# Moving a variance off VectorE, and loading a slot's weights one slot ahead, in a selective-scan kernel

## The chip, the cores and the metric

The kernel runs on one core of one Trainium2 chip. A core has a matrix engine (TensorE, PE in the profile), three engines for elementwise work (VectorE is DVE, ScalarE is ACT, GpSimd is POOL), and SyncE (SP), whose queue issues most of the transfers between HBM and the on-chip memory SBUF. TensorE writes its results to PSUM, a small memory in banks. Each engine takes its own instructions in order; semaphores order them across engines. The metric is the time of one execution on the device, in microseconds (us). Lower is better.

## What is computed

The input is 8 images of 128 x 128 tokens with 128 channels. Layer 0 is linear attention with a layer norm. Layer 1, where the change lies, expands each token to 256 channels (called `Cd` in the reference), runs a depthwise convolution, and then four scans over the image: by rows, by rows backwards, by columns, by columns backwards. Their sum is gated, normalised over the 256 channels and projected to 128. Cut to what matters:

```python
delta = softplus(dt_out + dbias)             # per channel and token
xc = exp(delta * A) * xc + (delta * u) * B   # the scan, token after token
y_k = xc * C + u * D                         # k = 0..3, one for each direction
y = y0 + y1 + y2 + y3                        # each turned back to the image's order
yz = y * silu(z)
mu = yz.mean(-1, keepdims=True)
var = ((yz - mu) ** 2).mean(-1, keepdims=True)
out = (gamma * (yz - mu) / sqrt(var + 1e-05) + beta) @ Wout
```

The kernel takes the variance as mean(yz^2) - mean(yz)^2, clamps it at zero and adds 1e-5.

## The kernel before

Three stages run one after the other: `layer0`, `layer1_front` (projection, convolution, the rows from which delta, B and C come) and `layer1_scan`. The change lies in the last one, which begins at about 4970 us of 9860 us. Inside the block `in_order` each engine's instructions keep the order in which the program writes them.

**Units, slots, images.** The scans are cut into 512 units of 1024 tokens (`CH`). Sixteen units in a row (`NCH`) make a slot: one image and one of its four directions. Four slots in a row add into one output image `o`, in a buffer `y` that holds the whole image; the first slot of an image has place 0. `step(n)` writes the work around unit n, with stages of neighbouring units interleaved by hand.

**A unit.** `load_rows` brings the rows that `delta` multiplies on TensorE by the slot's weights `dw` (L873, into a tile `px`, one of three in PSUM). ScalarE takes softplus of it (`soften`, L877), then exp (`decay`, L881). GpSimd multiplies delta into the input (`weigh`, L884). VectorE scans both halves of the channels (`scan`, L891 or L893). `spread` (L907) copies C over the partitions on TensorE, and in the next step `emit` (L919, L924, L931, L935) multiplies by it, with `gather` (L943, VectorE) and `add` (L950, GpSimd) adding to `y` in the slots of place 1 to 3. Softplus and exp need different activation tables, so each step has two table loads on ScalarE (counted under L877 and L881).

**Leaving.** When an image is complete, its 16 tiles of 1024 tokens leave one a step, while the first slot of the next image overwrites `y` behind them. For a tile: `gate` multiplies `y` by z one step ahead, one half on GpSimd and one on VectorE (L970); `square` (L973, ScalarE) squares it in place; `moments` (L983, TensorE) sums both over the channels; `keep` (L989, ScalarE) copies these rows from PSUM; `to_tokens` (L995, TensorE) turns them so that each token lies on a partition, in a tile `pq` of 8 means and 8 mean squares per partition; `variance` (L997 to L1003, VectorE) makes the variance; `deviation` (L1006, GpSimd, in the next step) raises it to -1/2; `project` (L1013, TensorE) multiplies by the output weights; `store` (L1019, VectorE, in the next step) scales by the deviation and sends the rows out. `moments`, `to_tokens` and the second `spread` share one PSUM buffer, called "pt", one after the other. A *leaving step* below is a step in which a tile passes `square` to `variance`: 7 x 16 of them beside scans and 16 more at the end, after the last scan.

**Weights.** A slot's weights are ten small transfers (`weights`, L813 and L814) into one of two buffers that alternate between slots. They stand in SyncE's queue just ahead of the rows of the slot's first unit, which is two steps ahead of that unit.

**Order in a step.** For VectorE in a leaving step: first scan, the stores of the tile ahead, second scan, the state (L901), the variance (L999 to L1003), the gate of the next tile (L970), then, in the next step's text, the two halves of the emit (L919). For ScalarE: both decays, both squares, `keep`, both softenings for the next unit. For GpSimd: `weigh` of the first half, `deviation`, `weigh` of the second half, `gate`, and in some steps a transfer that adds a part of the sums into `y` (L844).

Of the kernel before, what the change touches and what calls it, by code (L numbers as in the profile page):

```python
# [8 lines left out]
F32 = mybir.dt.float32  # L9
BF16 = mybir.dt.bfloat16  # L10
AF = mybir.ActivationFunctionType
ALU = mybir.AluOpType
# [4 lines left out]
P = 128  # L17
# [4 lines left out]
NC2 = 2  # L22
R = 8
K = 4
GW = 4
# [6 lines left out]
NCH = L // CH  # L32
EPS0 = 1e-3
EPS1 = 1e-5
# [26 lines left out]
@contextmanager  # L61
def in_order(tc):

    bb = tc.nc.cur_bb
    first = len(bb.bb.instructions)
    yield
    assert tc.nc.cur_bb is bb
    info = mybir.DependencyInfo(mybir.DependencyClass.NoSync, mybir.DependencyReason.DATA)
    last = {}
    for i in bb.bb.instructions[first:]:  # L70
        if i.engine in last:
            tc.add_manual_dep(i, last[i.engine].name, info, reason="in_order")
        last[i.engine] = i
# [614 lines left out]
def layer1_scan(ctx: ExitStack, tc, ubs, xps, zs, gs, dtw, dtb, a_log, gamma, beta, w_out, out):  # L688
# [15 lines left out]
    nc = tc.nc  # L704
# [3 lines left out]
    sm = ctx.enter_context(tc.tile_pool(name="l2s", bufs=4))  # L708
# [31 lines left out]
    half = const.tile([P, GW, 2], F32, name="half2")  # L740
    nc.vector.memset(half, -0.5)
    rws, dws = [], []
    for i in range(3):
        t = const.tile([P, CH], BF16, name=f"rows{i}")
# [3 lines left out]
    for i in range(2):  # L748
        t = const.tile([P, D2], BF16, name=f"dtw{i}")
# [83 lines left out]
    units = []  # L833
    for o in range(B):
        for s in ([3, 0, 1, 2] if o % 4 < 2 else [1, 2, 3, 0]):
            sl = Slot(len(units) // NCH, o, s)
# [9 lines left out]
    def load_rows(n):  # L846
        sl, i = units[n]
        m = sl.at(i)
        if i == 0:
            sl.weights()  # L850
        rw = rws[n % 3]
        md = NCH - 1 - m if sl.dt_turned_back else m
        src = xps[sl.dt_image, sl.dt_order].rearrange("j r l -> (j r) l")
        for j in range(3):
            nc.sync.dma_start(rw[3 * NR * j : 3 * NR * j + 3 * NR, :], src[:, md * CH : md * CH + CH])
        nc.sync.dma_start(rw[96:99, :], xps[sl.b, sl.order, :, R + 1, m * CH : m * CH + CH])

    def load(n):
        sl, i = units[n]
        m = sl.at(i)  # L860
        ubt[n] = wp.tile([P, NC2, CH], F32, name="ubt", tag="ub", bufs=4)
        nc.sync.dma_start(ubt[n], ubs[sl.b, sl.order].rearrange("c p l -> p c l")[:, :, m * CH : m * CH + CH])
# [16 lines left out]
    def decay(n, c):  # L879
        sl, i = units[n]  # L880
        nc.scalar.activation(da[n, c], sp[n, c], AF.Exp, scale=sa[:, sl.s, c : c + 1])  # L881

    def weigh(n, c):
        nc.gpsimd.tensor_tensor(ubt[n][:, c, :], ubt[n][:, c, :], sp.pop((n, c)), ALU.mult)  # L884

    def scan(n, c):
        sl, i = units[n]
        x, e = da[n, c], ubt[n][:, c, :]
        start = 0.0 if i == 0 else st[n - 1][:, c : c + 1]
        if sl.back:  # L890
            nc.vector.tensor_tensor_scan(e[:, ::-1], x[:, ::-1], e[:, ::-1], start, ALU.mult, ALU.add)  # L891
        else:
            nc.vector.tensor_tensor_scan(e, x, e, start, ALU.mult, ALU.add)  # L893
# [43 lines left out]
    def gather(n):  # L937

        sl, i = units[n]
        v = sl.y_at(i, 0)  # L940
        if sl.y_turned:
            v = v.rearrange("p c a b -> p c b a")
        nc.vector.tensor_tensor(v, v, ts.pop(n), ALU.add)  # L943
# [6 lines left out]
            nc.gpsimd.tensor_tensor(v[:, c], v[:, c], h[:, c], ALU.add)  # L950


    zt, rst, pts = {}, {}, {}

    def piece(m, hf):
        return y[:, :, (2 * m + hf) * GN : (2 * m + hf + 1) * GN]
# [15 lines left out]
    def square(m, hf):  # L972
        nc.scalar.activation(piece(m, hf), zt[m, hf], AF.Square)  # L973
# [17 lines left out]
    def to_tokens(m):  # L991
        sr = pts.pop((m, "rows"))
        pts[m] = p = pe.tile([P, GW, NC2, 2], F32, name="pq", tag="pt")
        for w in range(GW):
            nc.tensor.matmul(p[:, w], sr[:, w * H : w * H + H], sel, start=True, stop=True)  # L995

    def variance(m):  # L997
        mv = sm.tile([P, GW, NC2, 2], F32, name="mv")
        nc.vector.tensor_copy(mv, pts.pop(m))  # L999
        rst[m] = rstd = sm.tile([P, GW, NC2], F32, name="rstd")  # L1000
        nc.vector.tensor_tensor(rstd, mv[:, :, :, 0], mv[:, :, :, 0], ALU.mult)
        nc.vector.tensor_tensor(rstd, mv[:, :, :, 1], rstd, ALU.subtract)
        nc.vector.tensor_scalar(rstd, rstd, 0.0, EPS1, ALU.max, ALU.add)  # L1003

    def deviation(m):
        nc.gpsimd.tensor_tensor(rst[m], rst[m], half, ALU.pow)  # L1006

    def project(m, hf, bank):
        z = zt.pop((m, hf))
# [18 lines left out]
    for o in range(B):  # L1028
        n = (o + 1) * K * NCH
# [5 lines left out]
    N = len(units)  # L1035

    def step(n):
        live = 0 <= n < N
        then = n + 1 < N
        before = 1 <= n <= N  # L1040
        now, last, soon = (leaving.get(n + i) for i in (0, -1, 1))
        first = before and units[n - 1][0].place == 0
        if before:
            emit(n - 1, 0)
            if not first:
                gather(n - 1)
            emit(n - 1, 1)
        if n + 2 < N:
            load_rows(n + 2)
        if first and n + 3 < N:  # L1050
            load(n + 3)
        if live:
            for c in range(NC2):
                decay(n, c)
            weigh(n, 0)
        if last:
            deviation(last[1])
        if live:
            weigh(n, 1)
        if now:  # L1060
            for hf in range(2):
                square(now[1], hf)
            moments(now[1])
        if live:
            scan(n, 0)
            da.pop((n, 0))
        if last:
            for hf in range(2):
                store(*last, hf)
        if then:  # L1070
            for c in range(NC2):
                delta(n + 1, c)
        if now:
            keep(now[1])
        if then:
            for c in range(NC2):
                soften(n + 1, c)
        if now:
            to_tokens(now[1])
        if live:  # L1080
            scan(n, 1)
            state(n)
        if now:
            variance(now[1])
        if live:
            spread(n, 0, "pc")
            spread(n, 1, "pt")
        if soon:
            gate(*soon, 0, nc.gpsimd)
            gate(*soon, 1, nc.vector)  # L1090
        if now:
            p = da.pop((n, 1)) if live else px.tile([P, CH], F32, name="px")
            for hf in range(2):
                project(now[1], hf, p[:, hf * 512 : hf * 512 + 512])
        elif live and units[n][0].place == 0:
            da.pop((n, 1))
        if before and not first:
            add(n - 1)
        if n + 3 < N and not first:
            load(n + 3)  # L1100
        if n in summed:
            add_d(*summed[n])
        if n in fetched:
            fetch(*fetched[n])

    with in_order(tc):
        for n in range(2):
            load_rows(n)
        for n in range(3):
            load(n)  # L1110
        for c in range(NC2):
            delta(0, c)
            soften(0, c)
        for n in range(N + NCH + 1):
            step(n)
# [65 lines left out]
```

## Time and profile before

The time before is 9870.49 us, the median of 3 runs (9860.43 to 9883.38). The profiled execution spans 9860.3 us. What matters of it:

| part | what | us |
|---|---|---|
| scans L891 and L893, VectorE | 960 with a carried state, 64 without | 2355.3 |
| weigh L884, GpSimd | 1024, mean 2431 ns | 2442.4 |
| soften L877, ScalarE | 1024, mean 1024 ns, and 512 table loads of 1283 ns | 1035.4 + 656.9 |
| decay L881, ScalarE | 1024, mean 1109 ns, and 512 table loads of 1283 ns | 1103.1 + 656.9 |
| variance L999, L1001, L1002, L1003, VectorE | 128 each, means 165, 825, 677 and 223 ns | 242.1 |
| gate L970, VectorE half | 128, mean 1261 ns | 161.5 |
| deviation L1006, GpSimd | 128, mean 2326 ns | 297.8 |
| the seven leaving phases with scans | 112 steps | 1383.7 |
| after the last scan | 16 leaving steps | 150.3 |

The page gives an instruction a line of the kernel, an engine, its tiles (out<-in), its shape, how often it runs, and the engine's idle time just before it with what ended it. "Busy" includes the time in which an instruction has been started and waits inside for a memory port; only an idle gap says that an engine had nothing to start. An engine can therefore look full without working. Comparing the minimum, the median and the maximum of one shape shows such waiting.

### The profile page before, as it was taken

To read this page: it belongs to the slowest core of one execution; us is meant where nothing else is said; L and a number is where in the kernel's file an instruction comes from. 1 tells how busy PE (TensorE), PEld (TensorE's weight loads), DVE (VectorE), ACT (ScalarE), POOL (GpSimd) and SP (SyncE) were. 2 spreads that over 40 slices of the span, in tenths; PEclk is the share of its full clock that TensorE was granted. 3 is DMA by queue.
4 is the path that set the end of the run, shared out by engine and by line. 5 is a ranking of instruction groups with operands and counts; after the bars stand their busy time and mean duration, and the time that the engine had idled before them with its cause. 6 is when DMAs were issued, how large, how long until landed. Compare 5 with 4: busy or idle time off the path is not lost. (4 is left out here: it accounts for less than half of the span.)

```text
span 9860.3 us, 90189 instructions
## 1 busy us (share of the span) xinstructions
PE 6392.8 (65%) x24352; PEld 3116.9 (32%) x24352; DVE 8364.1 (85%) x9060; ACT 7121.7 (72%) x8098; POOL 7143.2 (72%) x4224
## 2 busy tenths in 40 slices
PE   8889999988787678766733644536345363543636
PEld 5555555553232223222200311304023040220403
DVE  6556775566898888888889999999999999999996
ACT  5556565556877777777778787787877878777784
POOL 3444554455584568766769899898988989889897
PEclk9999999999898889888855756757567585665857
DMA  2332223323675678877755957769486684866848
GB/s 91 130 129 108 85 109 128 131 101 140 218 229 211 226 259 240 233 250 255 259 164 159 261 157 219 211 171 254 151 230 197 179 249 152 246 182 192 236 152 216
DMA packets 1034809, 1851.22 MB, mean 188 GB/s; under 512 B 274852, under 2 KB 500772, under 8 KB 1026112
## 3 DMA queue, kind: packets, MB, share of 16 engines
q1 hardware_dynamic: 999488, 1711.23, 53.3%
q0 software_dynamic: 34816, 134.23, 7.1%
q8 instruction: 199, 3.26, 0.1%
q14 instruction: 306, 2.51, 0.1%
HBM read 1153.03 MB, written 692.12 MB: 187 GB/s over the span
## 5 line engine op out<-in xcount | busy, mean ns | idle before, releaser
L884 POOL TENSOR_TENSOR ubt<-ubt,sp 128x1024 f32<-128x1024 f32 x1024 | 2442.4, 2431 | 250.2 <-ACT sp L877 154.5
L873 PE MATMUL px<-rows,dtw 128*128 128x512 bf16 x2048 | 947.0, 564 | 2249.0 <-DVE y L943 1012.3
L504 POOL TENSOR_TENSOR tap<-tap 128x1024 f32<-128x1024 f32 x512 | 1206.6, 2366 | 717.3 <-ACT tap L502 617.6
L512 DVE SCALAR_TENSOR_TENSOR acc<-xb,cw,acc 128x1024 f32<-128x1024 f32 x1024 | 1320.7, 1290 | 51.1
L494 PE MATMUL acc<-xi,wt 128*128 128x512 f32 x2048 | 982.4, 624 | 571.9 <-ACT ures L519 571.6
L877 ACT ACTIVATE sp<-px 128x1024 f32<-128x1024 f32 x1024 | 1035.4, 1024 | 398.7 <-PE px L873 321.5
L950 POOL TENSOR_TENSOR y<-y,ubt 128x512 f32<-128x512 f32 x768 | 1154.2, 1537 | 149.1 <-DVE ubt L924 145.9
L873 PEld LDWEIGHTS <-dtw 128*128 128x128 bf16 x2048 | 169.8, 110 | 3078.1 <-issue 1021.0
L891 DVE TENSOR_TENSOR_SCAN ubt<-px,state,ubt 128x1024 f32<-128x1024 f32 x480 | 1106.5, 2336 | 6.6 <-issue 3.6
L893 DVE TENSOR_TENSOR_SCAN ubt<-px,state,ubt 128x1024 f32<-128x1024 f32 x480 | 1105.1, 2336 | 7.3 <-issue 3.6
L881 ACT ACTIVATE px<-sp,sa 128x1024 f32<-128x1024 f32 x1024 | 1103.1, 1109 | 6.1
L502 ACT ACTIVATE tap<-xb,cw 128x1024 f32<-128x1024 f32 x768 | 833.4, 1139 | 155.5 <-DVE acc L510 92.6
L877 ACT ACT_TABLE_LOAD x512 | 656.9, 1283 | 252.1 <-PE px L873 233.7
L494 PEld LDWEIGHTS acc<-xi,wt 128*128 128x128 f32 x2048 | 395.7, 198 | 1138.7 <-ACT ures L519 677.1
L274 POOL TENSOR_TENSOR q<-q,qs 128x512 f32<-128x512 f32 x256 | 271.2, 1060 | 666.5 <-DVE qs L273 666.5
L881 ACT ACT_TABLE_LOAD x512 | 656.9, 1283 | 9.1
L1013 PEld LDWEIGHTS px<-wg,z 128*128 128x128 f32 x4096 | 563.5, 221 | 118.8 <-issue 113.4
L907 PE MATMUL pc<-rows,csel 128*128 128x512 bf16 x1024 | 514.6, 583 | 82.9 <-DVE mv L999 80.0
L1013 PE MATMUL px<-wg,z 128*128 128x128 f32 x4096 | 563.3, 304 | 0.0
L467 PE MATMUL pxb<-xi,wi 128*128 128x512 f32 x1024 | 497.5, 608 | 29.0 <-ACT xh L607 24.7
L943 DVE TENSOR_TENSOR y<-y,px 128x1024 f32<-128x1024 f32 x384 | 468.6, 1220 | 14.2
L924 DVE TENSOR_TENSOR ubt<-ubt,pc 128x1024 f32<-128x1024 f32 x384 | 466.2, 1214 | 0.0
(159 smaller groups left out, 15071.0 us busy)
## 6 DMA issues: line engine op xcount, KB each, us to landing
ubt<-ubs SPq DMA_DIRECT2D x512, 1024.0 KB
zs<-z SPq DMA_DIRECT2D x512, 256.0 KB
ubs<-ures SPq DMA_DIRECT2D x256, 512.0 KB
ubs<-turned SPq DMA_DIRECT2D x256, 512.0 KB
y<-gs POOLq DMA_DIRECT2D x128, 1024.0 KB, 11.8
z<-zs SPq DMA_DIRECT2D x256, 512.0 KB
rows<-xps SPq DMA_DIRECT2D x1536, 60.0 KB
xi<-x SPq DMA_DIRECT2D x120, 576.0 KB
```

The source lines that it names most:

```text
L494: nc.tensor.matmul(acc[:, s, :], wt[:, j, c, :], x, start=(j == 0), stop=(j == len(ON_PE) - 1))
L502: nc.scalar.activation(t, at(n, c, *d), AF.Copy, scale=cw[:, c, tap(*d) : tap(*d) + 1])
L504: nc.gpsimd.tensor_tensor(sums[n, c], sums[n, c], t, ALU.add)
L512: nc.vector.scalar_tensor_tensor(acc, at(n, c, *d), cw[:, c, tap(*d) : tap(*d) + 1], acc, ALU.mult, ALU.add)
L873: nc.tensor.matmul(p[:, hf * 512 : hf * 512 + 512], sl.dw[:, c * P : c * P + P], src, start=True, stop=True)
L877: nc.scalar.activation(t, da[n, c], AF.Softplus)
L881: nc.scalar.activation(da[n, c], sp[n, c], AF.Exp, scale=sa[:, sl.s, c : c + 1])
L884: nc.gpsimd.tensor_tensor(ubt[n][:, c, :], ubt[n][:, c, :], sp.pop((n, c)), ALU.mult)
L891: nc.vector.tensor_tensor_scan(e[:, ::-1], x[:, ::-1], e[:, ::-1], start, ALU.mult, ALU.add)
L893: nc.vector.tensor_tensor_scan(e, x, e, start, ALU.mult, ALU.add)
L950: nc.gpsimd.tensor_tensor(v[:, c], v[:, c], h[:, c], ALU.add)
L1013: nc.tensor.matmul(po[:, w, :], z[:, c, w * H : w * H + H], wg[:, c, :], start=(c == 0), stop=(c == NC2 - 1))
```

## The change

The diff has two parts that have nothing to do with each other.

**Variance.** Before, VectorE copied `pq` out of PSUM, squared the means, subtracted and clamped: four instructions of 8 or 16 elements a partition. After, ScalarE squares the means straight from PSUM (`square_mean`, right after `to_tokens` in the step's text, and so behind both softenings in ScalarE's order), VectorE only subtracts that square from the mean square that it reads in PSUM, and GpSimd clamps and adds 1e-5 in `deviation`, ahead of the power. It is meant to take small work off VectorE. For each tile VectorE runs three instructions fewer, ScalarE one more, GpSimd one more; TensorE's are the same.

**Weights.** The ten transfers of a slot move from the queue's place ahead of its first rows to the second step of the slot before it, so that they don't stand between other transfers where a slot begins. The transfers themselves and their number stay.

```diff
@@ -846,8 +846,6 @@
     def load_rows(n):
         sl, i = units[n]
         m = sl.at(i)
-        if i == 0:
-            sl.weights()
         rw = rws[n % 3]
         md = NCH - 1 - m if sl.dt_turned_back else m
         src = xps[sl.dt_image, sl.dt_order].rearrange("j r l -> (j r) l")
@@ -950,7 +948,7 @@
             nc.gpsimd.tensor_tensor(v[:, c], v[:, c], h[:, c], ALU.add)
 
 
-    zt, rst, pts = {}, {}, {}
+    zt, rst, pts, mv = {}, {}, {}, {}
 
     def piece(m, hf):
         return y[:, :, (2 * m + hf) * GN : (2 * m + hf + 1) * GN]
@@ -994,16 +992,18 @@
         for w in range(GW):
             nc.tensor.matmul(p[:, w], sr[:, w * H : w * H + H], sel, start=True, stop=True)
 
+    def square_mean(m):
+        mv[m] = t = sm.tile([P, GW, NC2], F32, name="mv")
+        nc.scalar.activation(t, pts[m][:, :, :, 0], AF.Square)
+
     def variance(m):
-        mv = sm.tile([P, GW, NC2, 2], F32, name="mv")
-        nc.vector.tensor_copy(mv, pts.pop(m))
         rst[m] = rstd = sm.tile([P, GW, NC2], F32, name="rstd")
-        nc.vector.tensor_tensor(rstd, mv[:, :, :, 0], mv[:, :, :, 0], ALU.mult)
-        nc.vector.tensor_tensor(rstd, mv[:, :, :, 1], rstd, ALU.subtract)
-        nc.vector.tensor_scalar(rstd, rstd, 0.0, EPS1, ALU.max, ALU.add)
+        nc.vector.tensor_tensor(rstd, pts.pop(m)[:, :, :, 1], mv.pop(m), ALU.subtract)
 
     def deviation(m):
-        nc.gpsimd.tensor_tensor(rst[m], rst[m], half, ALU.pow)
+        rstd = rst[m]
+        nc.gpsimd.tensor_scalar(rstd, rstd, 0.0, EPS1, ALU.max, ALU.add)
+        nc.gpsimd.tensor_tensor(rstd, rstd, half, ALU.pow)
 
     def project(m, hf, bank):
         z = zt.pop((m, hf))
@@ -1077,6 +1077,7 @@
                 soften(n + 1, c)
         if now:
             to_tokens(now[1])
+            square_mean(now[1])
         if live:
             scan(n, 1)
             state(n)
@@ -1098,12 +1099,15 @@
             add(n - 1)
         if n + 3 < N and not first:
             load(n + 3)
+        if live and units[n][1] == 1 and n - 1 + NCH < N:
+            units[n - 1 + NCH][0].weights()
         if n in summed:
             add_d(*summed[n])
         if n in fetched:
             fetch(*fetched[n])
 
     with in_order(tc):
+        units[0][0].weights()
         for n in range(2):
             load_rows(n)
         for n in range(3):
```

## The prediction

> **What bounds the kernel now.** I read the page's totals first, then the chain of waits, then windows cut from the start of one unit's first scan to the start of the next (a step), then single instructions.
>
> ```profile
> PE 6392.8 (65%) x24352; PEld 3116.9 (32%) x24352; DVE 8364.1 (85%) x9060; ACT 7121.7 (72%) x8098; POOL 7143.2 (72%) x4224
> ```
>
> The windows below show, in order, a plain step, the last step of an image, and three steps in which a tile of 1024 tokens leaves (square, moments, variance, projection, store).
>
> ```profile
> core 0: us, PE busy (x) PEld busy (x) DVE busy (x) ACT busy (x) POOL busy (x), PEclk, DMA share, GB/s
> 5476.38:5484.60 8.22, 1.90 (x5) 0.44 (x4) 8.15 (x8) 6.77 (x6) 7.38 (x5) 0.50 1.04 274
> 5495.64:5509.95 14.31, 3.48 (x8) 0.94 (x10) 9.50 (x7) 6.66 (x7) 11.53 (x7) 0.50 0.66 169
> 5522.65:5533.87 11.22, 9.70 (x64) 5.75 (x62) 10.80 (x18) 9.17 (x10) 10.27 (x6) 1.00 0.97 286
> 5598.35:5609.80 11.45, 8.94 (x61) 6.58 (x60) 11.31 (x20) 9.09 (x9) 10.71 (x6) 0.85 0.96 255
> 5609.80:5625.34 15.54, 8.71 (x69) 6.11 (x68) 15.40 (x19) 9.41 (x10) 10.84 (x6) 0.99 1.01 287
> ```
>
> Plain steps are VectorE alone: 8.15 of 8.22 us, and the change does not touch them. Leaving steps look the same, 11.31 of 11.45 and 15.40 of 15.54, but part of that busy time is no work:
>
> ```profile
> L999 DVE COPY mv<-pq x128: 147/164/177, 5518.0 to 9850.4; 128x16 f32<-128x16 f32 x128
> L1001 DVE TENSOR_TENSOR rstd<-mv x128: 166/720/3094, 5518.3 to 9850.6; 128x8 f32<-128x8 f32 x128
> L1002 DVE TENSOR_TENSOR rstd<-mv,rstd x128: 166/167/3574, 5518.5 to 9850.8; 128x8 f32<-128x8 f32 x128
> L1003 DVE TENSOR_SCALAR rstd<-rstd x128: 171/171/2345, 5518.7 to 9851.0; 128x8 f32<-128x8 f32 x128
> ```
>
> The same eight elements take 166 ns or 3 us. The timeline says what the long ones wait for: they start again where a GpSimd instruction ends (first view VectorE, second GpSimd, same step).
>
> ```profile
> 5605.31 0.77 DVE L1001 TENSOR_TENSOR rstd<-mv 128x8 f32<-128x8 f32 x1
> 5606.12 0.17 DVE L1002 TENSOR_TENSOR rstd<-mv,rstd 128x8 f32<-128x8 f32 x1
> 5606.32 0.17 DVE L1003 TENSOR_SCALAR rstd<-rstd 128x8 f32<-128x8 f32 x1
> 5606.40 1.22 DVE L970 TENSOR_TENSOR z<-y,z 128x1024 f32<-128x1024 f32 x1
> ```
>
> ```profile
> 5603.72 2.34 POOL L884 TENSOR_TENSOR ubt<-ubt,sp 128x1024 f32<-128x1024 f32 x1 [0.22 <-issue]
> ```
>
> L1001 ends at 5606.08, when L884 has ended (5606.06). With the groups' means (825, 677, 223 ns) the blocked time is (825-166)+(677-166)+(223-171) = 1222 ns a tile, 156 us over 128 tiles.
>
> ScalarE is the other half of the picture. In the step of 11.22 us it never rests except for the moments:
>
> ```profile
> 5523.53 1.99 ACT L973 ACTIVATE y<-z 128x1024 f32<-128x1024 f32 x2
> 5527.51 0.59 ACT L989 COPY sr<-pm 128x512 f32<-128x512 f32 x1 [1.99 <-PE pm L983]
> 5528.12 1.28 ACT L877 ACT_TABLE_LOAD   x1
> 5529.41 1.94 ACT L877 ACTIVATE sp<-px 128x1024 f32<-128x1024 f32 x2
> 5531.37 1.28 ACT L881 ACT_TABLE_LOAD   x1
> 5532.66 2.15 ACT L881 ACTIVATE px<-sp,sa 128x1024 f32<-128x1024 f32 x2
> ```
>
> 1.99 + 1.99 + 0.59 + 1.28 + 1.94 + 1.28 + 2.15 = 11.22, the step. So ScalarE's round is 9.23 us plus the wait for the moments, and it is the floor of a leaving step already.
>
> **What the Trainium skill says.** "SBUF — State Buffer", Who interferes with whom: a VectorE instruction with two SBUF inputs, or in a two-port mode (tensor_scalar can be), locks out and is locked out by a GpSimd instruction reading SBUF, for the whole instruction. The trace agrees: L1001 to L1003 stretch, while L1019 with its data in PSUM has a mean of 340 ns. The same section lets an instruction with one SBUF input pass. The new subtraction (PSUM and SBUF) is free of the lock; **the next instruction, L970, has two SBUF inputs and is not**. "ScalarE: Activation LUTs", Table sets: a function of another set costs a table load. L973 squares behind Exp without one, and the changed program's instruction list has 128 more on ScalarE, none of them a load.
>
> **The change, part by part.**
>
> VectorE loses three instructions a tile: 0.17 + 0.17 + 0.17 and two to three gaps of 0.03, about 0.48 us behind the lock (L970 could start when L1001 now does: 8.0 to 7.5 us into the step in the 11.4 us steps). The copy (165 ns) is replaced by the subtraction at the same price.
>
> The lock wait moves to L970. Of the 112 leaving steps with scans, the timeline shows 66 where only L1001 is blocked (gain 0.48, if VectorE is the bound), 27 where L1002 or L1003 is blocked (the first got through, then a multiplication L884 took the lock), and 19 with none (all among an image's first three). In 15 of the 27, L970 would ask once and slip in where L1001 did, 2.4 to 3.9 us earlier, about 45 us together; the step of 15.54 us is one. These steps have a late GpSimd gate (z still in transfer, DMA share near 1), so part is lost again to the next transfer: I keep 60%, **-27**.
>
> ScalarE gains one square of 8 elements. Its nearest row is L718, 208 ns on the same shape; the ScalarE page (What ACT_TABLE_LOAD costs) gives 186 + 0.833 x 8 = 193 ns, each pointer operand 93 more. Bounds 0.10 (overlap of 93) and 0.29; I take 0.22. It stands behind both softenings and ahead of the two decays, the squares and so the next moments: all of it is on ScalarE's round. Round: 9.45 plus the wait. Now the step is 11.45 = 9.23 + 2.2; squares and the last emit (L919, which frees the moments' PSUM bank) end together, so TensorE does all moments afterwards. With L919 0.48 earlier and the squares 0.22 later, the wait is that of the 11.22 step, 1.99: 9.45 + 1.99 = 11.44. **VectorE's 0.48 us therefore buys nothing in the ordinary leaving step**; where TensorE's clock is low both waits stretch alike (12.35 us steps). I book 0 for these, -15 to +20 as bounds.
>
> The subtraction now waits for this square, which follows the softenings. Behind it on VectorE stand L970, both emits and the next scan; TensorE's second spread and projection wait for its PSUM bank. In ordinary steps the softenings end 6.2 us into the step, before VectorE is ready at 6.85: hidden. In an image's first three leaving steps they end at 8.7 to 10.4, and L970 then meets L884 running: 3.3 us late there. ScalarE sets those steps, so the lag is taken once, and the third or fourth is long now anyhow (14 to 16 us, waiting for z): **+5**.
>
> In the last leaving step (10.3 us, no L970 behind) the subtraction passes the lock and VectorE is free 1.2 us sooner; 7 x 1.0: **-7**.
>
> GpSimd gains a clamp of 8 elements: L300, half as wide, takes 190 ns; 0.19 to 0.39. Its power (mean 2326 ns, 1636 when not locked out by L970) moves little: now the clamp waits for L970 instead. GpSimd has 10.3 to 10.8 busy of 11.2 to 11.5, and the stores that need the result come 2.9 us later: 0.
>
> Weights: ten transfers leave the queue ahead of rows. Within an image the slot changes cost nothing now (the steps there run 8.16 to 8.23): no gain. At the seven image changes the queue's L813s stretch over 11.40 us (5487.98 to 5499.38) and the rows of the next unit follow; VectorE waits 4.81 us in the second window. Seven such windows are 14.31, 10.70, 14.06, 13.96, 14.28, 12.50, 12.57; the shortest is GpSimd's own 10.70 us of work, so at most 92.38 - 7 x 10.70 = 17.5. DMA is full just before, so not all: **-14**. The loads now fall in the second step of a slot; in a leaving phase they stand ahead of the z fetches with DMA share 0.97, up to 3 us an image, which the later z wait (4.64 us of GpSimd in the fourth step) mostly absorbs: **+3**.
>
> Tail (9710 to 9860): no scans; the square adds 0.2 to a chain of TensorE and DMA: **+2**.
>
> Sum: -27 + 5 - 7 - 14 + 3 + 2 = -38: **9832 us**.
>
> **Rivals.**
> - *VectorE's relief counts in full*: ScalarE has slack that I deny, since TensorE's moments start earlier. 66 x 0.48 = 32, second blocks 45, ends 8, weights 17, and the tail's power: about -105, 9765. For it: VectorE is 99% busy in most leaving steps. Against: the 11.22 sum closes without slack. A full 156 us cannot come, L970 inherits the lock.
> - *The detour over ScalarE costs more* (slower): 112 x 0.22 = 25 where the round is the bound, 19 steps at up to 3.3 us taken half, 31, and weights in the leaving phase 10, against 14 + 7 + 10 gained: +35, 9905. For it: the square is last on the busiest stretch, and L970 then always asks after L884 has started. Against: ordinary steps show the softenings done in time.
> - *Nothing measurable*: the second blocks come back as z waits and the weights' gain as later row waits: 9865.
>
> **How the numbers follow.** Forecast 0.45, full relief 0.17, slower 0.20, nothing 0.18. Under 9850.7 lie most of the forecast and the full relief: 0.59; within 0.2% part of the forecast and the last rival: 0.22; slower 0.19. For 8 in 10 the range reaches into both side cases: 9778 to 9898.
>
> **What would show it.** Right: L970's mean rises from 1261 ns to about 2 us with the blocked time of L1001 to L1003; VectorE's idle time in leaving steps grows while ScalarE shows only the moments' wait; ordinary leaving steps stay near 11.44; the steps over 13 us get rarer; the last step of an image comes near 10.7. Wrong: ordinary leaving steps of 10.9 (ScalarE not the bound), or VectorE waiting for the new square in every one of them (softenings later than I think), or more z waits in the second and third leaving steps.

## The result, and the profile after

| kernel | median us | range, runs | ratio to before, 95% interval |
|---|---|---|---|
| before, run beside it | 9875.86 | 9860.43 to 9883.38, 4 | |
| after | 9832.75 | 9824.68 to 9845.18, 4 | 0.9959 (0.9941 to 0.9978) |
| after, second time | 9840.83 | 9824.41 to 9848.81, 5 | 0.9963 (0.9950 to 0.9976) |
| after, third time | 9837.93 | 9820.76 to 9850.48, 5 | 0.9962 (0.9949 to 0.9975) |

The change makes the kernel 0.4% faster, 33 to 43 us by the three pairs of medians (beside the second and the third set, before had medians of 9873.94 and 9876.49). The prediction said 9832. The total is right; the terms of the sum are less so, and the rest of this text is about them.

First the totals of the page of after. VectorE's busy time has gone from 8364.1 to 8276.1 us.

```profile
PE 6386.5 (65%) x24352; PEld 3135.3 (32%) x24352; DVE 8276.1 (84%) x8676; ACT 7129.7 (73%) x8226; POOL 7184.2 (73%) x4352
```

Next the windows of the seven leaving phases, each from the first scan of its first step to that of the seventeenth. The last line adds them; the columns are those of the prediction's windows. Before:

```profile
sum 1383.74, PE 1063.64 PEld 738.20 DVE 1330.02 ACT 1038.68 POOL 1112.25; mean PE 151.95 PEld 105.46 DVE 190.00 ACT 148.38 POOL 158.89
```

After:

```profile
sum 1352.87, PE 1044.80 PEld 749.45 DVE 1254.49 ACT 1037.45 POOL 1142.79; mean PE 149.26 PEld 107.06 DVE 179.21 ACT 148.21 POOL 163.26
```

VectorE has 75.5 us less to do, the phases are only 30.9 us shorter, and the difference is rest: its idle time is 1383.74 - 1330.02 = 53.7 us before and 1352.87 - 1254.49 = 98.4 us after. More than half of what was taken off VectorE has become waiting.

The lines of after that answer to the four instructions of `variance` (instructions of one source line: count, shortest, median and longest in ns, first and last start):

```profile
L997 ACT ACTIVATE mv<-pq x128: 171/185/186, 5526.4 to 9813.1; 128x8 f32<-128x8 f32 x128
L1001 DVE TENSOR_TENSOR rstd<-pq,mv x128: 154/166/168, 5526.6 to 9813.3; 128x8 f32<-128x8 f32 x128
L968 DVE TENSOR_TENSOR z<-y,z x128: 1212/2180/4552, 5509.7 to 9806.1; 128x1024 f32<-128x1024 f32 x128
L1005 POOL TENSOR_SCALAR rstd<-rstd x128: 243/1219/1667, 5528.2 to 9813.6; 128x8 f32<-128x8 f32 x128
L1006 POOL TENSOR_TENSOR rstd<-rstd,half x128: 1657/1662/1671, 5529.4 to 9813.9; 128x8 f32<-128x8 f32 x128
```

The subtraction L1001, with one operand in PSUM, never takes over 168 ns: the 3 us stretches are gone from it. The gate L968 has them now: its shortest is 1212 ns, its median 2180. The clamp L1005 takes 243 ns when nothing is in its way and 1219 in the median, because it now stands where the gate is in its way; the power L1006 behind it is at its bare 1.66 us every time, where it had a mean of 2.3 us before. So the lock has been handed on twice, from the variance to the gate and from the power to the clamp.

The groups of VectorE in the last stage of after (busy us, mean ns | idle before, and what ended it) show where the rest comes from:

```profile
L968 DVE TENSOR_TENSOR z<-y,z 128x1024 f32<-128x1024 f32 x128 | 285.8, 2233 | 48.9 <-DMA z<-zs 48.6
L1001 DVE TENSOR_TENSOR rstd<-pq,mv 128x8 f32<-128x8 f32 x128 | 20.7, 162 | 82.1 <-ACT mv L997 81.3
```

VectorE waits 81.3 us for ScalarE's square, and 48.6 us for z where it was 7.1 before.

### The profile page after: what moved, and what is told of

Read it like the earlier page. It is cut to its first block, busy times and chain, and to the rows that moved or that the text cites. A ratio compares the mean times of both kernels' runs of the same rounds, so it can differ in the third digit from the quotient of the medians.

```text
span 9823.0 us, 89967 instructions
## 1 busy us (share of the span) xinstructions
PE 6386.5 (65%) x24352; PEld 3135.3 (32%) x24352; DVE 8276.1 (84%) x8676; ACT 7129.7 (73%) x8226; POOL 7184.2 (73%) x4352
## 5 line engine op out<-in xcount | busy, mean ns | idle before, releaser
L882 POOL TENSOR_TENSOR ubt<-ubt,sp 128x1024 f32<-128x1024 f32 x1024 | 2451.4, 2441 | 186.3 <-ACT sp L875 159.5
L502 ACT ACTIVATE tap<-xb,cw 128x1024 f32<-128x1024 f32 x768 | 833.2, 1139 | 155.4 <-DVE acc L510 92.4
L1013 PEld LDWEIGHTS px<-wg,z 128*128 128x128 f32 x4096 | 586.3, 228 | 163.9 <-issue 157.9
L1013 PE MATMUL px<-wg,z 128*128 128x128 f32 x4096 | 585.3, 312 | 0.0
## 6 DMA issues: line engine op xcount, KB each, us to landing
y<-gs POOLq DMA_DIRECT2D x128, 1024.0 KB, 11.9
```

The costliest lines, as they stand in the source:

```text
L502: nc.scalar.activation(t, at(n, c, *d), AF.Copy, scale=cw[:, c, tap(*d) : tap(*d) + 1])
L1013: nc.tensor.matmul(po[:, w, :], z[:, c, w * H : w * H + H], wg[:, c, :], start=(c == 0), stop=(c == NC2 - 1))
```

## Where it went, step by step

I cut the trace of every run at the starts of the first scans and added the 112 leaving steps with scans in three groups: the first four steps of the seven phases (28), the fifth to the fifteenth (77, "ordinary"), and the last (7). "Image change" is the seven steps just ahead of the phases. "Lock" is what the variance or the gate takes beyond its bare duration (170 and 1225 ns). All in us, from the profiled run of each.

| run | first four | ordinary | last | image change | lock | VectorE idle, leaving |
|---|---|---|---|---|---|---|
| before | 355.2 | 955.9 | 72.7 | 92.4 | 151.5 | 53.7 |
| after | 366.1 | 922.3 | 64.5 | 75.3 | 125.0 | 98.4 |
| after, 2nd | 372.5 | 930.0 | 65.3 | 77.5 | 140.9 | 98.0 |
| after, 3rd | 368.9 | 923.0 | 67.8 | 75.8 | 127.9 | 101.9 |
| e1, weights only | 358.2 | 954.3 | 74.3 | 75.8 | 160.6 | 47.2 |
| e2, variance only | 355.7 | 921.9 | 64.5 | 91.3 | 122.7 | 90.4 |
| e3, square on VectorE | 351.1 | 937.3 | 67.2 | 76.4 | 110.1 | 81.9 |
| e4, more on VectorE | 374.6 | 925.6 | 66.5 | 77.0 | 108.6 | 97.6 |
| e5, more on ScalarE | 362.2 | 922.4 | 70.9 | 75.9 | 125.8 | 98.8 |
| e6, weights later | 355.5 | 931.1 | 65.6 | 76.2 | 130.1 | 92.9 |
| e7, e6 and first squares on VectorE | 342.9 | 932.9 | 64.3 | 75.4 | 108.7 | 94.5 |
| e7, again | 342.1 | 929.0 | 65.4 | 76.2 | 110.2 | 89.2 |
| e8, without a sum | 329.3 | 887.0 | 66.1 | 74.6 | 117.0 | 40.7 |
| e9, gate without lock | 354.2 | 900.3 | 74.4 | 75.8 | 0 | 192.8 |

The three traces of after show what one trace is worth: 4 to 8 us in each of the first two columns. Before and most of the experiments have one trace, and it can stand at either end of its kernel's runs (that of e3 is the slowest of five), so differences of this size in one column prove nothing. The stages ahead of the last one, which no edit touches, end between 4993 (before) and 5017 us (after, 3rd), so totals of single traces compare worse than steps. From before to the first trace of after the stages ahead are 9.7 us longer, the leaving phases 30.8 shorter, the image changes 17.1, and all else 0.9 longer: together -37.3.

The ordinary steps gather at a few lengths, which turn out to tell more than the sums. Number of the 77 steps at each length (us); the rest lie between:

| run | 10.22 to 10.29 | 10.90 to 10.94 | 11.13 to 11.20 | 11.21 to 11.25 | 11.28 to 11.36 | 11.38 to 11.46 | 11.70 to 11.75 | 13.41 to 13.47 |
|---|---|---|---|---|---|---|---|---|
| before | 0 | 0 | 0 | 0 | 0 | 29 | 1 | 0 |
| after | 0 | 6 | 13 | 1 | 10 | 2 | 3 | 12 |
| after, 2nd | 0 | 5 | 16 | 1 | 10 | 0 | 5 | 9 |
| after, 3rd | 0 | 4 | 13 | 1 | 13 | 5 | 2 | 12 |
| e3 | 0 | 4 | 7 | 13 | 0 | 1 | 3 | 9 |
| e4 | 0 | 7 | 7 | 0 | 13 | 4 | 2 | 5 |
| e5 | 0 | 5 | 9 | 2 | 2 | 1 | 15 | 12 |
| e8 | 0 | 0 | 0 | 0 | 43 | 0 | 1 | 0 |
| e9 | 9 | 1 | 1 | 1 | 10 | 4 | 1 | 1 |

## The experiments

In the expectations, A is the prediction's own account and B the rival in which VectorE's relief counts in full. The kernel after ran again beside other runs, as a measure for them:

> The changed kernel once more, as the reference of this series. Theory A (ScalarE's round is the bound of an ordinary leaving step; the gain comes from second lock waits that are gone, from the last step of a leaving phase and from the weights): ratio 0.994 to 0.998, leaving phases together 1345 to 1362 us (1352.9 before this run, 1383.7 in the kernel before), last step of an image 10.6 to 10.9 us. Rival B (every instruction off VectorE shortens the step): the same.

> The changed kernel beside the one above: ratio 0.9955 to 0.9965, first four steps of the leaving phases 366 to 372 us together.

It gave 9840.83 and 9837.93 us (ratios in the first table), and the two further rows of the second.

### e1 and e2: each part alone

e1 is the kernel before with only the weights moved; e2 is after with the weights back:

```diff
     def load_rows(n):
+        if i == 0:
+            sl.weights()
...
-        if live and units[n][1] == 1 and n - 1 + NCH < N:
-            units[n - 1 + NCH][0].weights()
...
-        units[0][0].weights()
```

> Only the weights are moved; the variance is as before. Theory A: the seven last steps of an image fall from 92.4 to about 75 us together (10.6 to 10.9 each), the leaving phases stay at 1384 within 8 us, total -10 to -18 us, ratio about 0.9985. Rival C (the ten transfers now stand ahead of the z fetches in a leaving phase and delay them): the leaving phases grow by 10 to 25 us, mostly in their second to fourth steps, and the total is unchanged.

> Only the variance is changed; the weights are loaded as before. Theory A: the seven last steps of an image stay at about 92 us, the leaving phases fall by about 26 to 33 us as they did with both, total -23 to -33, ratio about 0.997. Rival B: the same or a larger gain. Rival C: the gain is larger than with both changes (over 40 us), since no weights delay the z fetches.

e1: 9865.70 us, 0.9992 (0.9984 to 1.0000), 8 us instead of the expected 10 to 18. e2: 9839.84 us, 0.9969 (0.9959 to 0.9980). The variance is nearly all of the gain; the weights alone are at the edge of what can be told from nothing. The leaving phases of e2 fell by 41.6 us, more than the expected 26 to 33 and more than in after (16 to 31): in this trace that is the sign of rival C.

The steps show why. e1 takes 16.6 us off the image changes, as much as after does. Windows of e1, the last step of the first image and the third step of its leaving phase:

```profile
core 0: us, PE busy (x) PEld busy (x) DVE busy (x) ACT busy (x) POOL busy (x), PEclk, DMA share, GB/s
5504.68:5515.96 11.28, 3.47 (x10) 0.92 (x10) 9.49 (x6) 6.66 (x7) 11.28 (x7) 0.65 0.75 201
5540.10:5553.50 13.40, 9.77 (x64) 5.75 (x64) 11.67 (x19) 11.35 (x12) 9.63 (x6) 0.98 0.98 291
```

The first is 14.31 before and 11.28 here, and GpSimd's busy time fills it: the weights no longer hold up the rows, and what stays is GpSimd's own work. But the third leaving step is 13.40, where the same step of before took 11.24. VectorE's timeline in it:

```profile
5547.46 0.17 DVE L1001 TENSOR_SCALAR rstd<-rstd 128x8 f32<-128x8 f32 x1
5548.95 2.01 DVE L968 TENSOR_TENSOR z<-y,z 128x1024 f32<-128x1024 f32 x1 [1.32 <-DMA z<-zs]
```

The z of this step comes late, with the ten weight transfers in the queue ahead of it: SyncE issues them from 5533.70 to 5539.30 us and the next two fetches of z from 5539.41. Over the seven phases the third step has a mean of 14.15 us (before 11.48) and the fourth 13.34 (before 14.86): part of the delay is absorbed one step later. Net, the first four steps cost e1 +3.0 us.

In e2 the first step rises from a mean of 13.11 to 14.84 and the fourth falls from 14.86 to 12.85, net +0.5. Together in after, the same two edits cost +10.9 to +17.3.

### e3: the square stays on VectorE, free of the lock

```diff
+        nc.vector.tensor_copy(mv, p[:, :, :, 0])
+        nc.vector.tensor_tensor(rstd, p[:, :, :, 0], mv, ALU.mult)
+        nc.vector.tensor_tensor(rstd, p[:, :, :, 1], rstd, ALU.subtract)
```

in `variance` with p the tile `pq`, and no `square_mean`. Every product has one operand in PSUM, so none meets the lock; VectorE has two small instructions more than after, ScalarE one less, and nothing waits for ScalarE.

> The changed kernel, but the mean is squared on VectorE again: a copy of the means from PSUM, a product of PSUM and that copy, and the subtraction, each with one SBUF input at most; the clamp stays on GpSimd. VectorE has two instructions (about 0.37 us) more in a leaving step than the changed kernel, ScalarE one fewer. Theory A: ScalarE's round loses its 0.09 us (ordinary clean steps 11.30 to 11.22) and VectorE no longer waits for the square in an image's first three leaving steps (1.6 + 0.4 + 0.5 us an image): the leaving phases fall by 12 to 25 us against the changed kernel, to about 1330 to 1340. Rival B: they grow by 0.37 x 112 = 41 us.

9829.28 us, 0.9953 (0.9939 to 0.9967). The first four steps are 15 to 21 us shorter than in after, the ordinary ones 7 to 15 longer: the leaving steps total 1355.6, within the spread of after (1352.9 to 1367.8). The expected 1330 to 1340 did not come, rival B's +41 neither. What the two kernels share, a variance that does not meet the lock and a clamp on GpSimd, is enough for the gain; the square need not leave VectorE. One part of theory A did come: the group of 10 to 13 steps at 11.28 to 11.36 us in after stands at 11.21 to 11.25 here, 0.07 less.

### e4 and e5: more work on VectorE, more work on ScalarE

e4 adds three copies of 16 elements out of PSUM to VectorE just ahead of the gate in each leaving step (167 ns each, 0.5 to 0.6 us together); e5 adds four squares of 8 elements to ScalarE right after the new one:

```diff
+        if now and live:
+            for j in range(3):
+                nc.vector.tensor_copy(sm.tile([P, 16], F32, name="pad", bufs=2), cps[n, 0][:, 0, 0:16])
...
+        for j in range(4):
+            nc.scalar.activation(sm.tile([P, GW, NC2], F32, name="pad", bufs=2), half, AF.Square)
```

> The changed kernel with three more VectorE copies of 16 elements from PSUM (about 0.165 us each, 0.6 us with the gaps, none of them able to take the lock) between the subtraction and the gate in each leaving step; their output is not used. Theory A (ScalarE's round sets the ordinary leaving step, VectorE's idle time of some 95 us in these steps and its lock wait hide the copies): leaving phases +0 to +15 us against the changed kernel (1353 and 1368 in two runs). Rival B (VectorE is the bound): 0.6 x 112 = +67 us.

> The changed kernel with four more squares of 8 elements on ScalarE right after the new one in each leaving step; their output is not used and no one waits for it. Each costs 0.09 us if they overlap as the first one did, up to 0.2 us. Theory A: ScalarE's round grows by 0.4 to 0.8 us and so do the ordinary leaving steps, +40 to +90 us over the leaving phases. Rival B: ScalarE waits over 2 us for the moments in each of these steps, which hides them: under +15 us.

e4: 9838.86 us, 0.9971 (0.9961 to 0.9981); ordinary steps 925.6, between the 922.3 and 930.0 of after. Given more work than the change has taken off, VectorE shows nothing of it there: 77 times 0.5 us would have been some 40. The lock wait fell to 108.6 us instead, since a gate that comes later waits less for the same GpSimd instruction to end.

e5: 9847.98 us, 0.9975 (0.9967 to 0.9983). ScalarE's timeline in one of its plain leaving steps (11.76 us):

```profile
5685.75 1.99 ACT L971 ACTIVATE y<-z 128x1024 f32<-128x1024 f32 x2
5689.73 0.59 ACT L987 COPY sr<-pm 128x512 f32<-128x512 f32 x1 [1.99 <-PE pm L981]
5690.34 1.28 ACT L875 ACT_TABLE_LOAD   x1
5691.63 1.94 ACT L875 ACTIVATE sp<-px 128x1024 f32<-128x1024 f32 x2
5693.46 0.18 ACT L997 ACTIVATE mv<-pq 128x8 f32<-128x8 f32 x1
5693.51 0.56 ACT L999 ACTIVATE pad<-half 128x8 f32<-128x8 f32 x4
5694.09 1.28 ACT L879 ACT_TABLE_LOAD   x1
5695.39 2.15 ACT L879 ACTIVATE px<-sp,sa 128x1024 f32<-128x1024 f32 x2
```

The only gap is still the 1.99 us for the moments, and the round from square to square (L971, 5685.75 to 5697.48) is 11.73 us, 0.43 longer than the 11.30 of after. In such steps ScalarE's round sets the length, as the prediction had it, and the table shows it for the whole group: 11.28 to 11.36 us in after, 11.21 to 11.25 without the square (e3), 11.70 to 11.75 with four more (e5).

But theory A's +40 to +90 us did not come. All 77 ordinary steps together are 922.4 us, no longer than in after, which is the number of its rival B, though not for its reason: the plain steps hide nothing, but most steps do not run at ScalarE's pace. The median of e5 lies 7 to 15 us above those of after, with intervals that overlap; so some of the load may show in the time, but this one trace doesn't say where. Its first four steps are shorter than after's by 4 to 10 us and its last longer by 3 to 6, both of which I leave open.

Which steps take the load without a trace? In after, 22, 22 and 18 of the 77 steps (three traces) are under 11.25 us, shorter than ScalarE's round, most at 10.91 and 11.17. They catch up: in the first trace 20 of the 22 stand right behind a step of 11.9 us or more. Such a step of after, 10.91 us from 5656.29, in lines of ScalarE, GpSimd and VectorE:

```profile
5658.58 0.58 ACT L987 COPY sr<-pm 128x512 f32<-128x512 f32 x1 [2.40 <-PE pm L981]
5661.58 2.35 POOL L882 TENSOR_TENSOR ubt<-ubt,sp 128x1024 f32<-128x1024 f32 x1 [0.98 <-ACT sp L875]
5663.04 0.16 DVE L1001 TENSOR_TENSOR rstd<-pq,mv 128x8 f32<-128x8 f32 x1
5663.11 1.90 DVE L968 TENSOR_TENSOR z<-y,z 128x1024 f32<-128x1024 f32 x1
```

ScalarE waits 2.40 us for the moments, so it is not what holds the step, and VectorE has no gap in it. VectorE's gate ends 1.08 us after GpSimd's multiplication. So it is in nearly all ordinary steps: in after, 72 of the 77 gates of the ordinary steps take over 1.5 us, and 65 of them end 1.08 to 1.12 us after a multiplication L882. Three small copies ahead of the gate (e4) then only shorten its wait, and the steps stay at 10.91 and 11.17 us in e3, e4 and e5 alike.

### e6 and e7: the two costs of the first four steps

e6 loads the weights at the fourteenth step instead of the second, in the slots in which a tile leaves in each step. e7 is e6 and squares the first three tiles of an image on VectorE:

```diff
+        late = NCH - 3 if live and units[n][0].place == 0 else 1
+        if live and units[n][1] == late and n - late + NCH < N:
+            units[n - late + NCH][0].weights()
...
+        if on_dve:
+            nc.vector.tensor_copy(t, mean_of)
+            nc.vector.tensor_tensor(t, mean_of, t, ALU.mult)
...
+            if n % NCH <= 2:
+                square_mean(now[1], True)
```

> The changed kernel, but in the slots of place 0 (the leaving phases) the next slot's weights are loaded in the fourteenth step instead of the second, where the transfer engines are busy 0.66 to 0.77 instead of 1.0. Theory D (the ten transfers ahead of the z fetches cost the third and fourth leaving step 1.5 to 2.5 us an image): the first four steps of the leaving phases fall from 366 to 372 us together to about 356, as with the variance alone, the last steps of an image stay at 75 to 78 us, total -10 to -16 us against the changed kernel. Rival A2 (that difference was the scatter of single runs): no change beyond 5 us.

> As the kernel with the late weights, and in addition the mean is squared on VectorE (copy and product from PSUM, no lock) in the first three leaving steps of an image, where VectorE waits for ScalarE's square; in the others on ScalarE. Theory A: the first leaving step falls from 14.7 to about 12.5 us and the second from 11.7 to 11.2, so -12 to -20 us against the kernel with late weights, ratio to the kernel before about 0.993. Rival: the lag is only moved to the fourth step, whose z comes when it comes: under 5 us.

> The kernel with late weights in place 0 and the first three squares on VectorE, once more beside the changed kernel on one chip. Theory A: 10 to 20 us faster than the changed kernel, ratio to the kernel before 0.994 to 0.996, first four steps of the leaving phases about 345 us together. Rival: the first result was a lucky chip, no difference to the changed kernel.

The first four steps: 366 to 372 with both costs (after), 355.5 without the early weights (e6; e2 has 355.7), 351.1 without the square behind the softenings (e3), 342.9 and 342.1 with neither (e7). So early weights cost 8 to 17 us and the late square 13 to 21, depending on what else is there. e6 gained nothing sure over after, 9827.88 us, 0.9958 (0.9946 to 0.9970). e7 gave 9815.19 us, 0.9949 (0.9937 to 0.9961), short of the expected 0.993, and again 9818.36, 0.9945 (0.9932 to 0.9957), where after on the same chip gave 9837.93: 20 us, as expected. Of the versions that leave nothing out it has the lowest medians, 0.10 to 0.18% ahead of after by the ratios, with intervals that still overlap.

VectorE's timeline shows the late square in the first leaving step. After (15.25 us):

```profile
5520.60 0.16 DVE L899 TENSOR_REDUCE state<-ubt 128x2 f32<-128x2 f32 x1
5526.61 0.17 DVE L1001 TENSOR_TENSOR rstd<-pq,mv 128x8 f32<-128x8 f32 x1 [5.86 <-ACT mv L997]
5526.70 2.46 DVE L968 TENSOR_TENSOR z<-y,z 128x1024 f32<-128x1024 f32 x1
```

The square it waits for, in ScalarE's timeline of the same step, comes straight behind the softenings:

```profile
5524.57 1.94 ACT L875 ACTIVATE sp<-px 128x1024 f32<-128x1024 f32 x2
5526.40 0.18 ACT L997 ACTIVATE mv<-pq 128x8 f32<-128x8 f32 x1
```

The same step in e7, second trace (12.33 us):

```profile
5526.57 0.16 DVE L899 TENSOR_REDUCE state<-ubt 128x2 f32<-128x2 f32 x1
5529.79 0.17 DVE L999 COPY mv<-pq 128x8 f32<-128x8 f32 x1 [3.07 <-PE pq L993]
5529.99 0.17 DVE L1000 TENSOR_TENSOR mv<-pq,mv 128x8 f32<-128x8 f32 x1
5530.19 0.17 DVE L1006 TENSOR_TENSOR rstd<-pq,mv 128x8 f32<-128x8 f32 x1
5530.27 1.22 DVE L968 TENSOR_TENSOR z<-y,z 128x1024 f32<-128x1024 f32 x1
```

In after the wait is 5.86 us and the gate then meets GpSimd as well (2.46 us). In e7 the wait is for `pq` alone, 3.07 us, and the gate slips through at its bare 1.22.

### e8 and e9: what holds the ordinary steps

e8 leaves out the term u * D of the sums (the calls of `add_d`, the transfers y<-gs). e9 replaces y by a tile in PSUM in the half of the gate that VectorE computes, so that half of the gated values are others; the gate then has one operand in SBUF and no lock.

```diff
-        if n in summed:
-            add_d(*summed[n])
```

```diff
-            gate(*soon, 1, nc.vector)
+            if live:
+                z = zt[soon[1], 1]
+                nc.vector.tensor_tensor(z, z, cps[n, 0].to_broadcast([P, NC2, GN]), ALU.mult)
+            else:
+                gate(*soon, 1, nc.vector)
```

> The changed kernel without the transfers that add a part of the sums into y (L844, 128 of 1 MB, seven of them in the first eleven steps of each leaving phase): the D term of 128 tiles is left out. GpSimd loses 1.2 us in the steps that had one, the transfer engines about a quarter of their load there. Theory E (the fifth to fifteenth leaving steps, 922 to 930 us for 77, are now long where the z of the next tile lands late and GpSimd's gate starts late, in 27 to 33 of the 77 steps): the late gates nearly vanish and these steps fall by 20 to 50 us. Theory F (the gate's lock wait and TensorE's projection make them long, not the transfers): under 10 us. The last steps of an image shorten to about 9.6 in both.

> The changed kernel, but VectorE's half of the gate multiplies z by a PSUM tile (the spread C of the running unit) instead of by y, so that it has one SBUF input: half of the gated values are replaced. Its lock wait (125 and 141 us in two runs) goes. Theory A (VectorE's waiting is hidden behind ScalarE's round and TensorE's moments and projection): the 77 ordinary steps keep a floor of 11.2 to 11.3 us, and fall by 0 to 30 us from 922 to 930. Rival B (the lock wait lies on the path): they fall by 60 to 90 us, to 10.9 us and less in the clean ones.

e8: 9730.92 us, 0.9857 (0.9842 to 0.9872), ordinary steps 887.0 and their median 11.30, where after has 11.73. Not one step past the first of a phase is over 13 us; after has 25. The gate on GpSimd shows what was in the way. After:

```profile
L968 POOL TENSOR_TENSOR z<-y,z 128x1024 f32<-128x1024 f32 x128 | 304.7, 2380 | 153.6 <-DMA z<-zs 86.8 <-DMA rows<-xps 28.9 <-PE px L1013 26.6
```

e8:

```profile
L968 POOL TENSOR_TENSOR z<-y,z 128x1024 f32<-128x1024 f32 x128 | 301.9, 2359 | 11.5 <-DMA z<-zs 6.7 <-PE px L871 4.4
```

With these 134 MB gone, z is there in time (86.8 to 6.7 us of waiting), and the step falls to the 11.30 us of ScalarE's round. e8 also spares GpSimd the issue of these transfers, some 1.2 us where it falls, and shortens the stretch from the start of the last unit to the end from 154.8 to 136.4 us; so not all of its 102 to 110 us against after is z. The forecast that the last step of an image shortens to 9.6 us did not come: the seven together take 74.6, 10.7 each.

Late z alone does not make the long steps. The commonest of them, about 13.44 us, twelve times in the first trace of after, has no wait for z in it. One of these, from 6160.92 us, in lines of GpSimd and VectorE:

```profile
6167.43 1.25 POOL L844 DMA_DIRECT2D y<-gs  x1
6168.29 2.79 POOL L882 TENSOR_TENSOR ubt<-ubt,sp 128x1024 f32<-128x1024 f32 x1
6167.76 4.42 DVE L968 TENSOR_TENSOR z<-y,z 128x1024 f32<-128x1024 f32 x1
```

VectorE's gate starts while GpSimd issues a transfer of the sums, and ends 1.1 us after the multiplication behind it. Of the ordinary steps over 13 us in the three traces of after (18, 19 and 17), 12, 11 and 8 are of this kind, with gates of 3.5 to 4.6 us. In all 31, GpSimd's gate of the same tile or of the one before had waited 1.8 us or more, most often for the transfer of z: late z puts GpSimd behind, its issue then falls where VectorE asks, and the lock does the rest. e8 takes z's delay and the issue away together, so it can't divide its 35 us between them.

e9: 9817.31 us, 0.9940 (0.9927 to 0.9954). Groups of VectorE and of GpSimd in it:

```profile
L1093 DVE TENSOR_TENSOR z<-z,pc 128x1024 f32<-128x1024 f32 x113 | 137.7, 1218 | 44.0 <-DMA z<-zs 32.6 <-PE pc L905 11.1
L1001 DVE TENSOR_TENSOR rstd<-pq,mv 128x8 f32<-128x8 f32 x128 | 21.1, 165 | 138.9 <-ACT mv L997 138.7
```

```profile
L968 POOL TENSOR_TENSOR z<-y,z 128x1024 f32<-128x1024 f32 x128 | 302.2, 2361 | 190.6 <-DMA z<-zs 118.9 <-DMA rows<-xps 43.0 <-PE px L1013 9.8
```

The last 125 to 141 us of lock in the leaving steps are gone, and the ordinary steps are only 22 to 30 us shorter. The rest went into waits for the square (81.3 to 138.7 us) and into 192.8 us of idle VectorE. Rival B's full relief was not to be had from this engine.

The sum of the ordinary steps is theory A's, its floor is not. 16 steps are under 11.0 us, nine of them at 10.22 to 10.29 with no gap of VectorE: this is what it needs when it meets no lock, where after had 10.91 and 11.17. The ten at 11.28 to 11.36 are ScalarE's again. And one step is left at 13.41 to 13.47, with a wait for z of its own, though the transfers are still there and z comes later than in after (118.9 us of waiting against 86.8): nine gates start while GpSimd issues one, take 1.22 us, and their steps have a mean of 11.36. So in the steps of 13.44 us it was the lock. In the 8 ordinary steps that are still over 13 us GpSimd's gate has waited 3.4 us and more.

## Why the prediction was right, and where not

- **VectorE's 0.48 us buys nothing in an ordinary leaving step**: right where ScalarE's round sets the step, 10 to 13 of 77 (e3, e5). As a floor for all of them that round was wrong. None of the 77 steps of before is under 11.39 us, so none was as short as ScalarE's 11.22; and after has 18 to 22 steps under 11.25, with 4 to 6 at 10.91, the 10.9 that the prediction itself named as a sign against it. There the relief did count: from 11.39 to 10.91 is 0.48, and from 11.39 to 11.17 it is 0.22; for 18 to 22 such steps that makes, by my estimate, 4 to 11 us. (The three 0.17 and two to three gaps of 0.03 that it adds up make 0.57 to 0.60; 0.48 is what the steps show.) What limits these steps is the gate's wait for GpSimd (e4, e9). The median of all 77 is 12.16 before and 11.73 after.
- **ScalarE's square 0.22 us on its round, 11.45 to 11.44**: mis-sized. L997 takes 185 ns, and as it follows the softplus at once, it begins before that one's recorded end. From the first softening's start to the next table load it is 1.96 us before (median) and 2.03 after: 0.07 net, less than the lower bound of 0.10. 9.23 + 0.07 + 2.00 = 11.30, as measured. Against the 11.45 of before that is -0.15 instead of -0.01. "Table sets" in the Trainium skill's "ScalarE: Activation LUTs" says that functions come in sets and only a change of set costs a load; this trace agrees, with 512 loads for each of the two functions as before.
- **The lock moves to the gate, 1261 ns to about 2 us**: right, 2233 ns. 149.3 us of lock in the variance became 125 to 141 in the gate. "Who interferes with whom" ("SBUF — State Buffer" in the Trainium skill) has the rule, and this trace agrees: L1001 with one SBUF input is free (at most 168 ns), L968 with two is not (up to 4552).
- **Second blocks -27**: the steps in which two instructions of the variance were blocked went from 15 (nine of them ordinary, six the fourth of a phase) to none, but the long steps did not go. Ordered by length, the 19 longest ordinary steps of before lost only 5 to 9 us together in the three traces of after, the other 58 lost 21 to 26. "Steps over 13 us get rarer" was wrong in this form: past the first of a phase there are 25 in the first trace of after, 26 before; those over 14 us fell from 11 to 4. The term took for granted that the gate, asking once, slips in. In 8 to 12 of the long steps it asks while GpSimd issues a transfer and waits 2.3 us and more (e8, e9). How much of the ordinary steps' 26 to 34 us is second blocks, no run takes apart.
- **First three leaving steps +5, weights in the leaving phase +3**: the step that failed. Alone neither costs more than was booked (e2 +0.5, e1 +3.0, each from one trace), and each was argued with the same reserve, the long fourth step that would absorb the delay. Together they cost 11 to 17 us, not 8: one reserve doesn't absorb both. And the slack itself was worth having, since without both (e7) these steps are 12 to 13 us shorter than before.
- **Last leaving step -7**: -5 to -8 in the three traces of after. **Image change -14**: -14.9 to -17.1, and the step of 14.31 us is 10.90, all of it GpSimd. **Clamp 0 and tail +2**: no cost of the clamp was seen, and the tail grew by 0 to 1.7 us (from the start of the last unit to the end, 154.8 before and 154.8 to 156.5 after).
- **The idle time of VectorE grows while ScalarE shows only the moments' wait**: the first is right (53.7 to 98.4). The second holds in the plain steps; in long ones ScalarE also waits for VectorE's gate, up to 0.59 us in the steps of 13.44.

So the ordinary steps, booked at -27 with some of it in the fourth steps, came out at -26 to -34; the image changes gave up to 3 us more than booked; the first steps were too hopeful by 3 to 9; and these cancelled. Added up, these terms come to -48, -29 and -40 us in the three traces of after, against the -38 that was booked. That 9832 met 9832.75 so closely is luck. Of the rivals, full relief is refuted by e4 and e9; the detour over ScalarE does cost something in the first steps (13 to 21 us, e3 against after and e7 against e6; the rival had 31), but not elsewhere.

## What to carry to other kernels

Taking a lock off one instruction hands it to the next that qualifies, so ask what stands behind it before booking the blocked time as gain; here 149 us of blocked time gave some 30. A step that catches up behind a longer one is not bound by the slowest round, so a floor read from one plain step is not the floor of all. When two edits each lean on the same slack, a later step that is long anyhow, book that slack once. And a small instruction moved to an idle engine costs little by its duration and much by its place: the same 0.18 us square cost 0.07 us in a plain step and some 2 us in the first step of a phase, because it stood behind the softenings.

## What I had not expected of the hardware

- The small square on ScalarE is cheaper than its duration where it directly follows another activation: 185 ns long, 0.07 us in the round. Four more added 0.43 us to it, at 0.56 us busy.
- On GpSimd the clamp of eight elements takes 243 to 1667 ns, and the power behind it always 1.66 us: the wait for the lock is borne by whichever instruction comes first, as on VectorE.
- Making VectorE's gate later (e4) lowered its lock wait by 16 to 32 us at no cost in the ordinary steps: a lock wait is partly only the place where slack is spent.
- A gate of VectorE that starts while GpSimd issues a transfer waits for the issue and for the multiplication behind it: 3.5 to 4.6 us, 31 times in three traces, against a bare 1.21 to 1.22.
